# A gated recurrence with ternary weights made beside it: new orders for ScalarE and VectorE, three weight buffers, and a half-width first product

## The chip, the cores and the metric

The kernel runs on one core of a Trainium2 chip. The metric is the device time of one execution in microseconds (us). Five engines work side by side, each through its own instructions in order: TensorE (PE in the profile, PEld for its weight loads), VectorE (DVE), ScalarE (ACT), GpSimd (POOL) and SyncE (SP), which in this kernel issues the DMA transfers. An instruction waits at the head of its engine's queue for what it needs, and all behind it wait too.

## The reference, cut to what matters

`x` is 2 sequences of 1024 tokens with 512 features. Four blocks add to it in turn: a gated recurrence (A), a feed-forward block with ternary weights, a differential attention, and the same feed-forward block again. The change lies in A and in the making of the ternary weights beside it.

```python
def block_a(x, w_in, w_out):                    # x is already layer-normalised
    q, k, v, a, g = split(x @ w_in.T, 5)        # 16 heads of 32
    q = q * rsqrt(mean(q * q, per head) + eps)
    k = tanh(k);  a = clip(sigmoid(a + 2.0), 0.6, 0.9995)
    u = k * v
    # in chunks of 64 tokens, with a state carried from chunk to chunk
    prefix = cumprod(a)
    states = prefix * (state + cumsum(u / max(prefix, 1e-6)))
    gate = sigmoid(g)
    return (gate * (q * states) + (1 - gate) * v) @ w_out.T

def ternary_quant(w):                           # bf16, groups of 64 weights
    scale = clip(mean(abs(w), per group), 1e-8)
    return clip(round(w / scale), -1, 1) * scale

def ffn(x):
    gate, up = split(x @ ternary_quant(w_gate_up).T, 2)
    return rms_norm(silu(gate) * up) @ ternary_quant(w_proj).T

x = x + block_a(layernorm(x));  x = x + ffn(layernorm(x))
x = x + block_b(layernorm(x));  x = x + ffn(layernorm(x))
```

## The kernel before, in words

**Tiles and blocks.** The 2048 tokens lie in the on-chip memory as 16 tiles `x` of 128 tokens by 512 features (`xres[i]` in the code). Stage A (L182 to L430) takes them in four blocks (`NBLK`) of 512 tokens, four tiles each (`TPB`). Per block a tile is normalised (`normal`, giving `xn`), turned by four transposes of TensorE into a bank of PSUM (`transposed`, giving `xnt`), and copied by ScalarE to the block's `a_xt`, features by tokens (`Input.turn`).

**One column group.** Within a block a loop runs over four groups `c` of 128 feature columns. TensorE computes the projections `kv` (with `w_k`, `w_v`) and `ag` (with `w_a`, `w_g`), four matmuls of 128x512 each, into pairs of PSUM banks, two of each kind. ScalarE makes `u`, `v`, `a` and `gate` from them. VectorE and GpSimd then do a chain: clip `a`, the prefix product (a scan), `u` divided by it, the state (a second scan, `mem`), times `qn`, minus `v`, times `gate`, plus `v`, which gives the column `yt`. `qn` is `q` times a factor that TensorE spreads over the heads with one small matmul (`pr`).

**Queries.** `queries` (L273) makes `q` of a block: four products `pq`, each followed by a copy and a square on ScalarE and by a matmul with `headmean` that adds the mean squares up (`pss`); then a root on ScalarE and the reciprocal, split into two parts, on VectorE (`rq_parts`). For the first block this stands ahead of the loop, for the others at the end of the block before. Then 16 matmuls `a_out` with `w_out` give the block's output, four per tile, and VectorE adds each tile's to `x`.

**Ternary weights.** Beside this the feed-forward weights are made ternary in 16 chunks `f` (class `Ternary`, L144): three transfers load a chunk (`w32`), ScalarE takes magnitude and sign (L157, L159), TensorE and ScalarE the mean of each group in three pieces (`mean`, L166 and L167), and VectorE finishes the chunk with six operations of 128x1536 (`finish`, L169 to L179). A transfer then stores it to DRAM (`w_kept`, L319). `quantise(i)` (L310) does piece `i` of the current chunk, 0 to 2 a mean and 3 the finish; the loop calls it at places that a tuple `pieces` lists. After a finish the next chunk is begun: its loads are issued and its magnitude and sign follow. There are two buffers of each kind.

**What follows.** `feed_forward` (L482) reloads all 16 chunks (L569) and takes the first block's normalised and turned tiles as `xs`, in two parts, high and low (class `FeedForwardInput`, L455). Its statistics (`ff_stats`) are taken in the last block of stage A, its tiles turned after it (L570 to L573). The first product is `g` (L524).

**What sets the order.** For TensorE the program's own order holds through stage A (`manual_schedule`, L323); for VectorE only while the first four tiles are normalised (L326). In all other places a scheduler of the framework orders each engine's instructions. SyncE issues transfers in the order it gets, and a transfer that waits holds the queue. Constants are laid by GpSimd in L213 to L240: `headmean`, `headrow`, two `rq_parts` and two `a_start`.

```python
        order = ExitStack()
        order.enter_context(tc.manual_schedule(engines={mybir.EngineType.PE}))
        ...
                if t < NBLK - 1:
                    pieces = ((2,), (), (3,)) if c % 2 else ((0,), (1,), ())
                else:
                    pieces = ((0, 1), (2,), (3,)) if c < NKC - 1 else ((), (), ())
```

Of the kernel before, what the change touches and what calls it, by code (L numbers as in the profile page):

```python
# [10 lines left out]
F32 = mybir.dt.float32  # L11
F32R = mybir.dt.float32r
# [5 lines left out]
P = 128  # L18
D = 512
# [23 lines left out]
def kernel(  # L43
# [37 lines left out]
    def load_x(lo, hi):  # L81
        for i in range(lo, hi):
            nc.sync.dma_start(out=xres[i], in_=x[ts(i, P), :])
# [55 lines left out]


# [3 lines left out]
    class Ternary:  # L144
# [3 lines left out]
        def __init__(self, pool, f, tiles):  # L148
            self.pool, self.f, self.n = pool, f, f"{f}_{tiles[0]}"
            self.shape = [P, len(tiles), D]  # L150
            self.w = pool.tile(self.shape, F32R, tag="w32", name=f"w32_{self.n}")
            w32 = self.w.bitcast(F32)
            for i, e in enumerate(tiles):
                src = w_pt[ts(f, P), :] if e == 2 else w_gu[e * NF + f].rearrange("p c n -> p (c n)")
                nc.sync.dma_start(out=w32[:, i, :], in_=src)
            self.mag = pool.tile(self.shape, BF, tag="mag", name=f"mag{self.n}")
            nc.scalar.activation(self.mag, w32, AF.Abs)  # L157
            self.sign = pool.tile(self.shape, BF, tag="sign", name=f"sign{self.n}")
            nc.scalar.sign(self.sign, w32)  # L159
            self.scale = None  # L160

# [20 lines left out]
    with ExitStack() as s:  # L182
# [15 lines left out]
        w_q, w_k, w_v = (load_w_in(i) for i in range(3))  # L198
# [8 lines left out]
        load_x(TPB, 2 * TPB)  # L207
        w_out = wa.tile([P, NKC, D], F32, name="w_out")
        nc.sync.dma_start(out=w_out, in_=w_out_t.rearrange("(c p) n -> p c n", p=P))

# [20 lines left out]
        for i in range(2):  # L231
            z = wa.tile([P, BLK], F32R, name=f"rq_parts{i}")
            nc.gpsimd.memset(z.bitcast(F32), 0.0)
            rq_parts.append(z)

        a_start = []
        for i in range(2):
            z = wa.tile([P, BLK], F32, name=f"a_start{i}")
            nc.gpsimd.memset(z, 0.0)
            a_start.append(z)  # L240
# [32 lines left out]
        def queries(t, xt):  # L273

            q = ap_.tile([P, NKC, BLK], F32, tag="q", name=f"q{t}")
            pss = bank(f"pss{t}")
            late = []

            def mean_square(c, sq):
                nc.tensor.matmul(  # L280
                    pss, headmean[:, c, :], sq, start=(c == 0), stop=(c == NKC - 1)
                )

            for c in range(NKC):
                pq = bank(f"pq{t}_{c}")
                project(pq, w_q, c, xt)
                nc.scalar.copy(q[:, c, :], pq)
                sq = ap_.tile([P, BLK], F32, tag="sq", name=f"sq{t}_{c}")
                nc.scalar.square(sq, pq)
                if late:  # L290
                    mean_square(*late.pop())
                late.append((c, sq))
                if c < 3 and t:
                    quantise(c)
                elif c and not t:
                    quantise(c - 1)
            mean_square(*late.pop())
            rq = ap_.tile([16, BLK], F32, tag="rq", name=f"rq{t}")
            nc.scalar.activation(rq, pss[:16, :], AF.Sqrt, bias=rms_eps[:16])
            nc.vector.reciprocal(rq, rq)  # L300
            parts = rq_parts[t % 2]
            hi, lo = parts[:16], parts[32:48]
            nc.vector.tensor_copy(hi, rq)
            nc.vector.tensor_sub(lo, rq, hi.bitcast(F32))
            quantise(3)
            return q, parts

        load_x(2 * TPB, NTT)

        def quantise(i):  # L310

            now = chunk[0]
            if now is None:
                return
            if i < 3:
                now.mean(i, bank)
                return
            now.finish(now.w)
            nc.sync.dma_start(out=w_kept[now.f].bitcast(F32), in_=now.w.bitcast(F32))  # L319
            chunk[0] = Ternary(tp, now.f + 1, range(3)) if now.f + 1 < NF else None  # L320

        order = ExitStack()
        order.enter_context(tc.manual_schedule(engines={mybir.EngineType.PE}))  # L323
        before = [None] * NKC
        first = Input(0, at_once=False)
        with tc.manual_schedule(engines={mybir.EngineType.DVE}):  # L326
            for j in range(TPB + 1):
                if j < TPB:
                    first.measure(j)
                if j:  # L330
                    first.normal(j - 1)
                    first.turn(j - 1)
        xt = first.xt
        q, rq = queries(0, xt)
        for t in range(NBLK):
            yt = wa.tile([P, NKC, BLK], F32, tag="yt", name=f"yt{t}")
            following = None
            for c in range(NKC):
                n = f"{t}_{c}"
                kv, ag = big(f"kv{n}"), big(f"ag{n}")  # L340
                project(kv[:, 0, :], w_k, c, xt)
                project(kv[:, 1, :], w_v, c, xt)

                if t < NBLK - 1:
                    pieces = ((2,), (), (3,)) if c % 2 else ((0,), (1,), ())
                else:
                    pieces = ((0, 1), (2,), (3,)) if c < NKC - 1 else ((), (), ())
                for i in pieces[0]:
                    quantise(i)
                project(ag[:, 0, :], w_a, c, xt)  # L350
                project(ag[:, 1, :], w_g, c, xt)
                for i in pieces[1]:
                    quantise(i)
                if following and c > 1:
                    for j in (2 * c - 4, 2 * c - 3):
                        following.turn(j)
# [9 lines left out]
                other = nc.gpsimd if (t, c) < (NBLK - 1, NKC - 1) else nc.vector  # L366
# [12 lines left out]


# [6 lines left out]

                pr = bank(f"pr{n}")
                nc.tensor.matmul(pr, headrow[:, c, :], rq, start=True, stop=True)
                qn = ap_.tile([P, BLK], F32, tag="qn", name=f"qn{n}")  # L390
                nc.vector.tensor_mul(qn, pr, q[:, c, :])
# [4 lines left out]

                if t + 1 == NBLK and c == 0:
                    ff_stats = layernorm_stats(range(TPB), "f0_0")
                if t + 1 < NBLK and c < 2:
                    if c == 0:  # L400
                        following = Input(t + 1)
                    following.normal(0 if c == 0 else 1)
                for i in pieces[2]:
                    quantise(i)
                if following and c == 2:
                    following.normal(2)
                    following.normal(3)

            if following:
                xt = following.xt  # L410
                q_next, rq_next = queries(t + 1, xt)
            products = [(j, k) for j in range(TPB) for k in range(NKC)]
            if not following:

                order.close()
                products.sort(key=lambda jk: jk[1] == NKC - 1)
            po = {}
            for j, k in products:
                if k == 0:
                    po[j] = bank(f"a_out{t}_{j}")  # L420
                nc.tensor.matmul(
                    po[j], yt[:, k, ts(j, P)], w_out[:, k, :], start=(k == 0), stop=(k == NKC - 1)
                )
                if k == NKC - 1:
                    xi = xres[t * TPB + j]
                    nc.vector.tensor_add(xi, xi, po[j])
                    if following:
                        quantise(j)
            if following:
                q, rq = q_next, rq_next  # L430

    edge_sb = ctx.enter_context(tc.tile_pool(name="edge", bufs=1, reuse_waits="tile"))
# [20 lines left out]
    class FeedForwardInput:  # L455


        def __init__(self, which, t, pool, tag, stats=None):
            self.n = f"{which}_{t}"
            self.which, self.tiles = which, range(t * TPB, (t + 1) * TPB)  # L460
            self.stats = stats or layernorm_stats(self.tiles, f"f{self.n}")
            self.xs = pool.tile([P, 2, NKC, BLK], F32R, tag=tag, name=f"xs{self.n}", bufs=1)
            self.xn = {}

        def normal(self, j):
            i = self.tiles[j]
            self.xn[j] = normal(i, j, self.stats, f"f{self.which}_{i}")

        def tile(self, j, psum):
            if j not in self.xn:  # L470
                self.normal(j)
            pt = transposed(self.xn.pop(j), f"f{self.which}_{self.tiles[j]}", psum)
            hi, lo = (self.xs[:, e, :, ts(j, P)] for e in range(2))
            nc.scalar.copy(hi, pt)  # L474
            nc.vector.tensor_sub(lo, pt, hi.bitcast(F32))

# [5 lines left out]
    def feed_forward(which, store, first=None, beside=None):  # L482


        with ExitStack() as s:
# [84 lines left out]
            if not first:  # L570
                first = FeedForwardInput(which, 0, edge_sb, "xt", ff_stats)
                for j in range(TPB):
                    first.tile(j, ring)  # L573
# [44 lines left out]
        0, False, None,  # L618
# [533 lines left out]
```

## Time and profile before

| | us |
|---|---|
| time, median of 3 runs | 2147.88 (2146.33 to 2148.32) |
| time of the profiled execution | 2146.65 |
| its span | 2144.9 |
| mean granted clock of TensorE in it | 0.996 of full speed |

By stretches the trace has, in microseconds busy:

| stretch | TensorE | VectorE | ScalarE | GpSimd |
|---|---|---|---|---|
| 0 to 20, first tiles | 11.79 | 6.88 | 6.29 | 5.76 |
| 20 to 90, queries and block 0 | 67.58 | 48.39 | 36.05 | 17.38 |
| 90 to 165, block 1 begins | 74.00 | 52.12 | 30.46 | 13.93 |
| 165 to 240 | 71.85 | 48.31 | 34.97 | 14.32 |
| 240 to 316 | 74.27 | 56.69 | 29.95 | 22.35 |
| 316 to 400, last block | 77.04 | 62.41 | 25.49 | 17.87 |
| 400 to 2144, all the rest | 1732.23 | 794.25 | 672.00 | 358.19 |

The span runs from the first instruction of the profiled execution to its last; the execution's own time has some two microseconds around it. A stretch is read by holding an engine's busy time against its length: TensorE lacks 8.2 us in the first, 2.4 in the second, 7.0 in the last of stage A. What ended such a gap is in the view of waits, which names the instruction that waited and the one that released it. An engine's busy time says nothing of whether anyone waits for it.

### The profile page before, as it was taken

What the parts mean: (1) busy time and instruction counts of PE and PEld (TensorE: products, weight loads), DVE (VectorE), ACT (ScalarE), POOL (GpSimd) and SP (SyncE); (2) the same over time, 40 slices, a digit from 0 to 9 for tenths busy, and PEclk for the clock granted to TensorE, in tenths of its full rate; (3) what the DMA queues carried; (4) which work ended last, traced back from release to release, by engine and by line L of the source; (5) the groups of instructions that cost most, each with busy time, mean ns of one, the idle gap of its engine ahead of it and who ended that gap; (6) DMA issues with size and microseconds to landing.
All of it is one profiled execution on the core that took longest, in us unless ns stands there. A gap on an engine that the chain in (4) does not pass through costs nothing.

```text
span 2144.9 us, 28054 instructions
## 1 busy us (share of the span) xinstructions
PE 2108.8 (98%) x10615; PEld 1242.2 (58%) x10624; DVE 1069.1 (50%) x2272; ACT 835.2 (39%) x1590; POOL 449.8 (21%) x812
## 2 busy tenths in 40 slices
PE   8999999999999999999999999999999999999998
PEld 3444444688888854444444444444545447888887
DVE  5766686533343234555555465464546662433322
ACT  4444333234344322444444422243434523333333
POOL 1312212122122221111111113021212221121212
PEclk9999999999999999999999999999999999999999
DMA  6111211600000111111110101201110033000000
GB/s 255 59 59 62 86 59 74 250 1 1 1 1 1 35 46 37 41 26 41 23 44 21 46 8 37 57 20 42 24 32 15 14 111 132 20 1 20 1 20 20
DMA packets 50999, 98.71 MB, mean 46 GB/s; under 512 B 10800, under 2 KB 19120, under 8 KB 50864
## 3 DMA queue, kind: packets, MB, share of 16 engines
q1 hardware_dynamic: 50864, 96.93, 13.8%
q8 instruction: 83, 1.36, 0.3%
q14 instruction: 52, 0.43, 0.1%
HBM read 58.75 MB, written 16.78 MB: 35 GB/s over the span
## 4 chain that ended last, share of the span: by engine, by line
PE 83%; DVE 8%; DMA 4%; ACT 2%; issue 1%; POOL 1%; SPq 1%; DVEq 0%; ACTq 0%; POOLq 0%
PE y L904 12%; PE g L524 11%; PE u L524 11%; PE f_out L545 11%; PE s L805 10%; PE pq L737 8%; PE t L866 8%; PE pv L702 3%; PE b_out L965 2%; DMA w<-in_w_pt_dram 1%; DMA w_kept<-w 1%; DVE one L174 1%; PE kv L269 1%; DVE w L179 1%; PE ag L269 1%
## 5 line engine op out<-in xcount | busy, mean ns | idle before, releaser
L882 ACT ACTIVATE pr<-t 128x512 f32<-128x512 f32 (+3 forms) x768 | 314.8, 497 | 380.6 <-PE t L874 380.4
L815 DVE CUSTOM_DVE_ANT_0 s<-s,causal 128x128 f32<-128x128 f32 (+3 forms) x512 | 245.3, 510 | 126.1 <-PE s L805 117.4
L904 PE MATMUL y<-pr,val 128*64 128x512 f32 (+3 forms) x1536 | 291.6, 501 | 0.2 <-POOL pr L885 0.2
L539 POOL TENSOR_TENSOR ssq<-ssq,sq 128x512 f32<-128x512 f32 x120 | 155.9, 1299 | 603.6 <-ACT sq L538 603.6
L530 DVE TENSOR_TENSOR h<-h,u 128x512 f32<-128x512 f32 x128 | 88.0, 688 | 362.0 <-PE u L524 355.9
L524 PE MATMUL g<-xs,w 128*128 128x512 f32 x1024 | 262.4, 398 | 0.9 <-ACT xs L474 0.7
L545 PE MATMUL f_out<-w,hs 128*128 128x512 f32 x1024 | 257.7, 394 | 0.3 <-DVE hs L533 0.3
L820 DVE TENSOR_REDUCE nmax<-s 128x1 f32<-128x512 f32 x256 | 165.0, 686 | 184.4 <-PE s L805 184.3
L524 PE MATMUL u<-xs,w 128*128 128x512 f32 x1024 | 256.4, 392 | 0.0
L805 PE MATMUL s<-gr,gr 32*128 32x512 f32 (+3 forms) x1536 | 248.8, 492 | 2.6 <-DVE nmax L815 2.6
L524 PEld LDWEIGHTS u<-xs,w 128*128 128x128 f32 x1024 | 192.4, 188 | 43.5
L545 PEld LDWEIGHTS f_out<-w,hs 128*128 128x128 f32 x1024 | 191.6, 188 | 43.9 <-DVE hs L533 1.1
L524 PEld LDWEIGHTS g<-xs,w 128*128 128x128 f32 x1024 | 190.9, 189 | 44.0 <-ACT xs L474 0.9
L866 PE MATMUL t<-gr,gr 32*128 32x512 f32 (+3 forms) x1536 | 198.8, 533 | 0.0
L904 PEld LDWEIGHTS y<-pr,val 128*64 128x64 f32 x1536 | 93.5, 136 | 179.9 <-issue 105.7
L737 PE MATMUL pq<-b_xt,w_qk 128*128 128x512 f32 x384 | 176.0, 603 | 0.0
L805 PEld LDWEIGHTS s<-gr,gr 32*128 32x128 f32 x1536 | 147.6, 185 | 46.8 <-issue 14.0
L532 ACT CAST hs<-h 128x512 fp32r<-128x512 f32 x128 | 79.4, 621 | 236.6 <-DVE h L530 236.6
L885 POOL TENSOR_SCALAR_AFFINE_SELECT pr<-pr 128x256 f32<-128x256 f32 x256 | 101.3, 408 | 332.2 <-ACT pr L882 332.2
L529 ACT ACTIVATE h<-g 128x512 f32<-128x512 f32 x128 | 76.5, 598 | 224.3 <-PE g L524 224.1
L533 DVE TENSOR_TENSOR hs<-h,hs 128x512 fp32r<-128x512 f32 x128 | 88.6, 692 | 83.1 <-ACT hs L532 83.1
L737 PEld LDWEIGHTS pq<-b_xt,w_qk 128*128 128x128 f32 x384 | 69.6, 189 | 88.0 <-issue 74.0
(155 smaller groups left out, 2211.0 us busy)
## 6 DMA issues: line engine op xcount, KB each, us to landing
w<-w_kept SPq DMA_DIRECT2D x32, 768.0 KB, 8.7
w_kept<-w SPq DMA_DIRECT2D x16, 768.0 KB, 3.2
gr<-gr SPq DMA_DIRECT2D x96, 128.0 KB, 2.3
w<-in_w_gu_dram SPq DMA_DIRECT2D x32, 256.0 KB, 2.8
share<-ys SPq DMA_DIRECT2D x128, 64.0 KB, 2.0
w_in<-in_w_in_t_dram SPq DMA_DIRECT2D x5, 1024.0 KB, 11.2
x<-in_x_dram SPq DMA_DIRECT2D x16, 256.0 KB, 7.1
w<-in_w_pt_dram SPq DMA_DIRECT2D x16, 256.0 KB, 3.5
```

The source lines that it names most:

```text
L524: nc.tensor.matmul(po, ws[f][:, part, ts(k, P)], xs[:, e, k, :], start=(k == 0 and e == 0), stop=(k == NKC - 1 and e == 1),)
L533: nc.vector.tensor_sub(hp[:, 1, :], h, hp[:, 0, :].bitcast(F32))
L539: nc.gpsimd.tensor_add(ssq, ssq, sq)
L545: nc.tensor.matmul(po[j], hp[:, e, ts(j, P)], ws[f][:, 2, :], start=(f == 0 and e == 0), stop=(f == NF - 1 and e == 1),)
L737: nc.tensor.matmul(po, w[:, k, ts(kind, P)], xts[b][:, k, ts(e, BLK)], start=(k == 0), stop=(k == NKC - 1),)
L805: nc.tensor.matmul(part, queries[:, ts(j, P)], keys[:, first : first + nk], start=True, stop=True,)
L815: nc.vector.tensor_tensor_reduce(part, part, causal[:, BLK - part.shape[-1] :], -1.0, 3.0e38, ALU.add, ALU.min, top,)
L820: nc.vector.tensor_reduce(top, part, AX.X, ALU.max, negate=True)
L866: nc.tensor.matmul(banks[u, e][:, :nq], keys[:, ts(kb, P)], queries[:, (qb + 1) * BLK - nq : (qb + 1) * BLK], start=True, stop=False,)
L882: nc.scalar.activation(pr[:, e, :nq], banks[u, e][:, :nq], AF.Exp)
L885: nc.gpsimd.affine_select(out=pr[:, :, :P], in_=pr[:, :, :P], compare_op=ALU.is_ge, fill=0.0, base=0, pattern=[[0, 2], [1, P]], channel_mu ...
L904: nc.tensor.matmul(y[64 * e : 64 * e + 64, lo:], all_values[:, HV * (NH * kb + h) : HV * (NH * kb + h) + 64], pr[:, e, : BLK - lo], start= ...
```

## The change

1. **VectorE's order.** Through all of stage A the program's order now holds for VectorE as well as for TensorE, until the stage's end. To suit it, the text is rearranged: the tiles of the next block are turned before `w_a`, not after `w_g`; `pr` and `qn` stand before the second scan; `qn` is written over `q`; the normals of the next block stand in the chain.
2. **The first four tiles.** ScalarE's order is given there instead of VectorE's own block. The first product of queries is made in two halves of 256 tokens; the first matmul of it stands before the fourth tile is turned.
3. **Constants.** `rq_parts` and `a_start` are set by VectorE instead of GpSimd.
4. **Three buffers of ternary weights.** `Ternary` is split: the loads come with the object, magnitude and sign with `begin`. Chunks 0, 1 and 2 are loaded at the start, chunk 1 ahead of `w_out`, chunk 2 behind it; chunk `f + 3` is loaded when `f` is finished. The loads of tiles 8 to 15 of `x` come after the first queries.
5. **Queries in parts.** The last mean square and the root (`roots`) and the reciprocal (`factors`) are called later, behind other products.
6. **The end of the stage.** The first feed-forward block's input is made inside the last block: nine statistics and two normals after column 1 (`c == 1`), the turns around `w_a` of column 3. Chunk 15's finish, and so its store, comes after all products. `w_q` and `w_k` share the memory that `xs` takes later. The 16 products of the last block are sorted by `max(k, 1)`.

```diff
+            self.w = pool.tile(self.shape, F32R, tag="w32", name=f"w32_{self.n}", bufs=3)
...
+        def begin(self):
+            pool, w32 = self.pool, self.w.bitcast(F32)
...
+        w_qk = edge_sb.tile([P, 2, NKC, D], F32, tag="xt", name="w_in_qk")
+        w_q, w_k = w_qk[:, 0], w_qk[:, 1]
...
+        chunk.append(Ternary(tp, 1, range(3)))
         w_out = wa.tile([P, NKC, D], F32, name="w_out")
         nc.sync.dma_start(out=w_out, in_=w_out_t.rearrange("(c p) n -> p c n", p=P))
+        chunk.append(Ternary(tp, 2, range(3)))
...
-            nc.gpsimd.memset(z.bitcast(F32), 0.0)
+            nc.vector.memset(z.bitcast(F32), 0.0)
...
-            nc.gpsimd.memset(z, 0.0)
+            nc.vector.memset(z, 0.0)
...
-            chunk[0] = Ternary(tp, now.f + 1, range(3)) if now.f + 1 < NF else None
+            chunk.pop(0)
+            if chunk:
+                chunk[0].begin()
+            if now.f + 3 < NF:
+                chunk.append(Ternary(tp, now.f + 3, range(3)))
...
-        order.enter_context(tc.manual_schedule(engines={mybir.EngineType.PE}))
+        fixed = {mybir.EngineType.PE, mybir.EngineType.DVE}
+        order.enter_context(tc.manual_schedule(engines=fixed))
...
+        def begin(half, k):
+            cols = ts(half, BLK // 2)
+            nc.tensor.matmul(
+                begun[:, cols], w_q[:, k, :P], first.xt[:, k, cols],
+                start=(k == 0), stop=(k == NKC - 1),
+            )
+
+        with tc.manual_schedule(engines={mybir.EngineType.Activation}):
             for j in range(TPB + 1):
                 if j < TPB:
                     first.measure(j)
                 if j:
                     first.normal(j - 1)
                     first.turn(j - 1)
+                if j == 3:
+                    begin(0, 0)
+        for k in range(1, NKC):
+            begin(0, k)
+        for k in range(NKC):
+            begin(1, k)
+        chunk[0].begin()
...
+                if not last:
                     pieces = ((2,), (), (3,)) if c % 2 else ((0,), (1,), ())
                 else:
-                    pieces = ((0, 1), (2,), (3,)) if c < NKC - 1 else ((), (), ())
+                    pieces = (((0, 1), (2,), (3,)), ((0, 1), (2,), ()), ((), (), ()))[max(c - 1, 0)]
+                project(kv[:, 0, :], w_k, c, xt)
+                if t + c == 0:
+                    roots()
+                    factors()
+                project(kv[:, 1, :], w_v, c, xt)
+                if t + c == 0:
+                    quantise(3)
+                if not last and c > 1:
+                    for j in (2 * c - 4, 2 * c - 3):
+                        following.turn(j)
+                        if c == 2:
+                            following.normal(j + 2)
                 for i in pieces[0]:
                     quantise(i)
+                ff_tiles = range(TPB) if last and c == NKC - 1 else ()
+                turn = lambda name: bank(name)
+                for j in ff_tiles[:2]:
+                    ff_first.tile(j, turn, j + 2)
                 project(ag[:, 0, :], w_a, c, xt)
+                for j in ff_tiles[2:]:
+                    ff_first.tile(j, turn)
                 project(ag[:, 1, :], w_g, c, xt)
...
                 other.tensor_add(yt[:, c, :], mem, v)
...
                 for i in pieces[2]:
                     quantise(i)
...
+                if last and c == NKC - 3:
+                    ff_first = FeedForwardInput(0, 0, edge_sb, "xt")
+                    ff_first.normal(0)
+                    ff_first.normal(1)
...
-                products.sort(key=lambda jk: jk[1] == NKC - 1)
+                products.sort(key=lambda jk: max(jk[1], 1))
...
                     nc.vector.tensor_add(xi, xi, po[j])
-                    if following:
+                    if not last:
+                        if j == 0:
+                            roots()
+                        elif j == 1:
+                            factors()
                         quantise(j)
-            if following:
+            if last:
+                quantise(3)
+            if not last:
                 q, rq = q_next, rq_next
+                following = Input(t + 2) if t + 2 < NBLK else None
+        order.close()
```

## The prediction

> **What bounds the kernel now.** The page comes first. TensorE is busy for nearly the whole span, so only what changes its work, its waits or its clock can move the time.
>
> ```profile
> PE 2108.8 (98%) x10615; PEld 1242.2 (58%) x10624; DVE 1069.1 (50%) x2272; ACT 835.2 (39%) x1590; POOL 449.8 (21%) x812
> ```
>
> The changed program's instruction order after the first `g` product equals the old one but for a few semaphore waits, so only the first 400 us matter. The view of waits for TensorE over 0 to 420 us lists what can be won there (total, times, longest):
>
> ```profile
> PE xnt_a L136 <- DVE xn_a L127: 7.5, 3, 6.8
> PE pm L166 <- ACT mag L157: 4.7, 2, 2.7
> PE pss L280 <- ACT sq L289: 3.4, 5, 2.1
> PE pq L269 <- ACT a_xt L265: 2.6, 4, 0.7
> PE xnt_f L136 <- DVE xn_f L127: 2.3, 2, 1.9
> PE a_out L421 <- POOL yt L395: 1.0, 1, 1.0
> ```
>
> About 23 us in all, 6.8 of them the unavoidable first load. VectorE's 50% is a mean: the view by stretches has it at 32.8 of 40 us in 360 to 400. The third resource is SyncE's queue, which issues in order. Its timeline around the stage's end, and TensorE's:
>
> ```profile
> 361.89 15.17 SPq L319 DMA_DIRECT2D w_kept<-w  x2
> 377.17 19.11 SPq L569 DMA_DIRECT2D w<-w_kept  x16
> ```
>
> ```profile
> 392.43 1.02 PE L421 MATMUL a_out<-w_out,yt 128*128 128x512 f32 x2
> ...
> 398.59 0.50 PE L524 MATMUL g<-xs,w 128*128 128x512 f32 x1 [0.68 <-ACT xs L474]
> ```
>
> The reader should see that the first ternary weights are asked for at 377.2, right behind the last store (376.7), and so are there long before `g` needs them at 398.6. The DMA view of that stretch gives 5.6 us from issue to landing for the first load.
>
> **Start.** VectorE takes over four memsets of 128x512. None is in the trace there: from its 128x1 (0.06 us) and 128x64 (0.11) each is about 0.49, an estimate; POOL's same memset took 0.52. Four end near 3.5 us, as the first `x` lands (3.56), and cost nothing; were they twice as long, the start would slip by 2 us. Off POOL they stop disturbing the first `xn_a`:
>
> ```profile
> 5.35 1.32 DVE L127 TENSOR_SCALAR xn_a<-x,mv_a,rstd_a 128x512 f32<-128x512 f32 x1
> 5.41 0.98 POOL L239 MEMSET a_start<- 128x512 f32 x2
> ```
>
> The median of these is 0.55, so the transposes begin 0.77 earlier. ScalarE's order lets copies 0 and 1 pass `rstd` 2 and 3, but the half product then meets its weights: `w_in0`, issued at 2.67, landed 7.6 later, at 10.3. So: first half matmuls 10.3 to 11.15, the fourth tile's transposes to 12.15, then 14 half matmuls. Before, `pq` began at 12.38; five matmuls took 0.855 and the rest 0.43, so its first column ended near 17.95. The slow rate lasted 4.4 us. If it lasts 4.4 from 10.3, six halves at 0.43 and eight at 0.215 end at 16.4: **1.6 us won**. The Trainium skill, "TensorE: Matmul & The Clock Gate" (Part 1), says that the window of 3.4 us is free-running; then the slow rate ends 3.4 to 6.8 us after the start, and the gain is 2.0 to 0.4. I take the row, and the rule for the range.
>
> **Middle.** Turning tiles before `w_a` removes the wait for `a_xt` at three block ends (0.63, 0.64, 0.63 in TensorE's timeline). The last mean square now stands behind a product: 4 waits of 0.32. With three buffers and chunks 1 and 2 loaded ahead of `w_out`, chunk 1's `mag` is no longer late (2.06 at 39.9); the 16 later transfers of `x` give way, and nobody needs them for 60 us. The waits of 2.07 (203.7) and 0.68 (295.2) also come from ScalarE's queue holding a `mag` whose load was late. Together 8.0 us.
>
> Against it stands VectorE's written order. One chunk's finish, from its timeline:
>
> ```profile
> 110.76 0.56 DVE L171 TENSOR_SCALAR scale<-scale 128x1536 bf16<-128x1536 bf16 x1 [4.44 <-ACT scale L167]
> 111.36 1.76 DVE L174 SCALAR_TENSOR_TENSOR one<-scale,mag 128x1536 bf16<-128x1536 bf16 x1
> 113.15 0.96 DVE L176 TENSOR_TENSOR scale<-scale,mag 128x1536 bf16<-128x1536 bf16 x1
> 114.14 0.96 DVE L177 TENSOR_TENSOR scale<-scale,mag 128x1536 bf16<-128x1536 bf16 x1
> 115.14 0.96 DVE L178 TENSOR_TENSOR scale<-scale,one 128x1536 bf16<-128x1536 bf16 x1
> 116.13 1.76 DVE L179 TENSOR_TENSOR w<-scale,sign 128x1536 fp32r<-128x1536 bf16 x1
> ```
>
> That is 7.1 us undisturbed, 7.9 at the stage's means. A column's chain (clip, scan, factors, scan, two products) is 7.9 from the busy times of its rows and its two waits for POOL (0.75 and 1.4), which the scheduler used to fill with pieces of the other and which now stand idle. At each of the first three block ends VectorE does: last chain, ended 8.7 after `ag`; a finish, 7.9; a wait of 2.1 for ScalarE (which holds `mag` until that finish lets its buffer go); a second finish, 7.1; only then the first `x` addition, 0.7. Sum 26.5. TensorE reaches the matmul that needs the bank this addition frees after 0.43 + 4x3.43 + 3x(0.86+0.21) + 2x3.43 + 1.07 = 25.3. So it waits about 1.2, 3.7 for three ends. **Middle: 4.3 won**, between 8.0 (VectorE quicker by 1.3) and about nothing.
>
> **Last block, the centre of the sum.** TensorE's work from its first `kv` to the last `a_out`, transposes included, is 8x6.87 + 9x0.21 + 4x0.43 + 4x0.52 + 32x0.43 = 74.4. In the trace this stretch plus waits runs from 316.13 to 398.59: 82.5. New, counted from its start:
> - VectorE gets `a` of column 0 at 15.1. Then in fixed order: chain 7.9, chunk 13's finish 7.9, chain 7.9, chunk 14's finish 7.9, nine statistics 7.0 (0.8 a pair at 23 us), reciprocal and two normals 1.3. The second normal is ready at 55.0; TensorE wants the first at 51.3.
> - Column 2's chain with one statistic, 9.1, then normal 0.55, `xs` 0.69, normal 0.55: 65.9. TensorE needs these for tiles 2 and 3, between `w_a` and `w_g`; `w_g` starts at 66.5 instead of 56.8: **9.7 lost**. ScalarE, POOL and `yt` queue behind the same chain but are not later than TensorE.
> - `w_g`, `pr` and 32 products: 17.6, to 84.1. `yt` of the last column comes at 78.9, in time for the four products that now stand last; the old wait of 1.0 is gone.
> - Chunk 15's finish now stands behind the last `x` addition: 0.1 + 0.69 + 7.1 + a statistic 0.66 = 8.6, to 92.7. SyncE's queue has that chunk's store ahead of all 16 weight loads, and the store waits. Store and issue 0.6, landing 5.6: `g` starts at 98.9. **14.8 of waiting**, covered before by the store having gone out 17 us earlier.
>
> 98.9 against 82.5 is 16.4 lost. The earlier `xnt_f` and `xs` waits are in the 82.5.
>
> **Clock.** The granted clock by stretches, around a wait of 2.7 us (352.4 to 355.1) and one of 1.95 (to 397.3); it is the third number from the end, before the DMA share and GB/s:
>
> ```profile
> 354.00:356.00 2.00, 0.94 (x3) 0.57 (x3) 1.82 (x3) 2.00 (x2) 0.90 (x1) 0.68 0.00 0
> 356.00:358.00 2.00, 2.00 (x4) 0.88 (x3) 1.01 (x1) 2.00 (x5) 0.95 (x1) 0.50 0.04 8
> ```
>
> The reader should see 0.68 and 0.50: half speed for some 3 us. It cost 1.1 us in `ag` (8.17 for 7.03) and 2.2 at `g` (eight matmuls in 4.07 for 1.87). The same page of the skill (the table "Why this matters") warns only of gaps above about 3 us; here gaps of 2 to 2.7 did it, so the trace decides. By the rule the new waits (3.2, 5.5) give one slow window, 1.7; by the row 2.2. I take **2.0**. The 14.8 gives another at `g`, where one was already.
>
> Sum: -1.6 - 4.3 + 16.4 + 2.0 = **+12.5**. On the profiled execution's 2146.65 (span 2144.9 and 1.75 around it) that is 2159; the median shown is 1.2 higher, 2160.4. I say 2160.
>
> **Rivals.** A measurement here tells some 0.2% (4.3 us) from no change.
> - *VectorE is not late at the end.* Speaks for it: it idled a third of most stretches. Against: before, chain plus finish took 15.2 to 15.9 us per column there (ends at 348.7, 364.5, 379.8), already interleaved. Without the 9.7 and the 2.0: +0.8, about 2148. Chance 0.11.
> - *The weight loads don't stand behind the store.* Place: SyncE's queue after chunk 14; it decides as soon as one load is issued before the last `x` addition. Price: 14.8 and the slow `g` (2.2) gone: -4.5, 2143, faster. Against: the order is fixed in the program, and 361.9 to 376.7 shows this queue waiting 14.4 us for VectorE. Chance 0.07.
> - *VectorE is also late in blocks 1 and 2*, so that finishes contend with POOL (one 2.70 and scale 1.49 where POOL ran, 88 to 93): 8.9 per finish instead of 7.9 adds about 2 per block end and 2 at the end: +20, 2168. Chance 0.14.
> - *The half product does nothing*, for its weights land late: +14, inside the forecast's range.
>
> Forecast 0.68. Its own range, with the last block's VectorE 10% quicker to 8% slower, and the bounds above, is 2152 to 2167; 2150 to 2168 holds 8 in 10. Slower 0.82, same 0.11, faster 0.07.
>
> **What would show it.** Right: `pq` with 256 columns from about 10.3; no wait of `pm` for `mag` near 40; `w_kept` and the 16 loads issued only after the last `a_out`, a gap of 13 to 16 us before `g`, and waits of `xnt_f` on `xn_f` of some 8 to 10 in all. Wrong: loads issued before the last addition, or `xnt_f` without waits.

## The result, and the profile after

The changed kernel takes 2163.68 us (median of 4 runs, 2161.07 to 2166.22), the kernel before 2147.57 beside it. The ratio is 1.0076, with a 95% interval of 1.0058 to 1.0093: slower by 16 us. The profiled execution took 2163.43, its span 2161.7, at a mean granted clock of 0.992 (0.996 before).

Four stretches make up the span, cut at places that both programs pass, each read from TensorE's timeline (the second query product ends where the first `pss` starts):

| stretch | before | after | difference | predicted |
|---|---|---|---|---|
| start to the end of the second query product | 21.53 | 19.25 | -2.28 | -1.6 |
| from there to the last block's first `kv` | 294.60 | 294.99 | +0.39 | -4.3 |
| from there to the first `g` | 82.46 | 101.38 | +18.92 | +18.4 (16.4 and clock 2.0) |
| from there to the end of the span | 1746.31 | 1746.08 | -0.23 | 0 |

The view of TensorE's waits over 0 to 420 us (total, times, longest), after the change:

```profile
PE g L583 <- DMA w<-w_kept: 14.4, 1, 14.4
PE xnt_f L136 <- DVE xn_f L127: 10.0, 3, 7.3
PE xnt_a L136 <- DVE xn_a L127: 7.5, 3, 6.0
PE a_out L496 <- ACT rq L344: 3.6, 3, 1.3
PE pm L196 <- DVE x L501: 2.9, 3, 1.0
PE pss L320 <- ACT sq L330: 0.6, 3, 0.2
```

The waits for `mag`, for `a_xt` and for `yt` are gone, as intended. Four others have come or grown, and 24.4 us of them lie in the last block. There VectorE's timeline (start, duration) reads:

```profile
357.05 2.71 DVE L204 SCALAR_TENSOR_TENSOR one<-scale,mag 128x1536 bf16<-128x1536 bf16 x1
359.79 1.91 DVE L206 TENSOR_TENSOR scale<-scale,mag 128x1536 bf16<-128x1536 bf16 x1
...
371.26 0.67 DVE L109 BATCH_NORM_STATS2 st_f<-x 128x6 f32<-128x512 f32 x1
371.84 0.99 DVE L127 TENSOR_SCALAR xn_f<-x,mv_f,rstd_f 128x512 f32<-128x512 f32 x2
```

and TensorE's and SyncE's:

```profile
372.43 1.97 PE L136 MATMUL xnt_f<-ident,xn_f 128*128 128x128 f32 x8 [7.32 <-DVE xn_f L127]
374.19 5.63 PE L308 MATMUL ag<-a_xt,w_in 128*128 128x512 f32 x8
381.79 0.66 PE L136 MATMUL xnt_f<-ident,xn_f 128*128 128x128 f32 x4 [1.97 <-DVE xn_f L127]
...
415.62 3.75 PE L583 MATMUL g<-xs,w 128*128 128x512 f32 x8 [14.37 <-DMA w<-w_kept]
```

```profile
346.37 63.45 SPq L361 DMA_DIRECT2D w_kept<-w  x3
409.93 13.41 SPq L628 DMA_DIRECT2D w<-w_kept  x13
```

VectorE is busy without a break from chunk 14's finish through all the statistics, and only then makes the normals that TensorE has been waiting for since 365. Of the nine statistics there the program's text asks for four at this place; ScalarE's root of these four is ready at 369.47, and its reciprocal comes on VectorE only at 371.18, behind statistics of later blocks. So some 1.7 of the 7.3 is not chunk 14's finish. The eight products after that wait run slow (5.63 for 3.60). SyncE's three stores, the last waiting for chunk 15's finish, hold its queue from 346 to 410; the first reload goes out at 409.93 and `g` starts 5.7 later.

### The profile page after: what moved, and what is told of

It is laid out like the page before. It is cut to its first block, busy times and chain, and to the rows that moved or that the text cites. A ratio compares the mean times of both kernels' runs of the same rounds, so it can differ in the third digit from the quotient of the medians.

```text
span 2161.7 us, 28045 instructions
## 1 busy us (share of the span) xinstructions
PE 2109.4 (98%) x10623; PEld 1245.4 (58%) x10632; DVE 1079.1 (50%) x2276; ACT 833.4 (39%) x1588; POOL 448.7 (21%) x808
## 4 chain that ended last, share of the span: by engine, by line
PE 90%; DVE 5%; DMA 2%; ACT 1%; POOL 1%; issue 1%; SPq 1%; DVEq 0%; ACTq 0%; POOLq 0%
PE y L959 12%; PE g L583 11%; PE u L583 11%; PE f_out L604 11%; PE s L860 10%; PE pq L792 8%; PE t L921 8%; PE ag L308 4%; PE kv L308 4%; PE pv L757 3%; PE b_out L1020 2%; PE a_out L496 2%; PE mt L900 1%; PE t L929 1%; DVE one L204 1%; DMA w<-w_kept 1%
## 5 line engine op out<-in xcount | busy, mean ns | idle before, releaser
L583 PE MATMUL g<-xs,w 128*128 128x512 f32 x1024 | 262.3, 398 | 14.4 <-DMA w<-w_kept 14.4
```

Source lines behind the costliest of these rows:

```text
L583: nc.tensor.matmul(po, ws[f][:, part, ts(k, P)], xs[:, e, k, :], start=(k == 0 and e == 0), stop=(k == NKC - 1 and e == 1),)
```

## The experiments

The times are medians; the kernel before, run beside them, took 2147.7 to 2148.1.

**e1, the last store on another queue.** Edit, in `quantise`:

```diff
+            queue = nc.gpsimd if now.f == NF - 1 else nc.sync
-            nc.sync.dma_start(out=w_kept[now.f].bitcast(F32), in_=now.w.bitcast(F32))
+            queue.dma_start(out=w_kept[now.f].bitcast(F32), in_=now.w.bitcast(F32))
```

> The changed kernel, but chunk 15's store is issued from GpSimd's queue, so that SyncE's queue goes straight from chunk 14's store to the weight loads. My theory: the 14.4 us that `g` waits in the changed kernel is SyncE's queue standing at that store, for the first load itself needs only memory that is free some 100 us earlier. Then the wait of `g` for `w<-w_kept` falls to under 1 us, its slow first product (3.75 for 2.06) becomes fast, and the waits of `xnt_f` stay at 10.0: 2163.7 - 14.4 - 1.7 = about 2147.5. Rival: the load waits for memory that stage A still holds, or for the channel; then the wait of `g` stays over 10 us and the time over 2159.

Measured: 2152.83 (ratio 1.0023, 1.0013 to 1.0034), 10.9 below the changed kernel. Its view of waits:

```profile
PE xnt_f L136 <- DVE xn_f L127: 10.8, 3, 7.3
...
PE f_out L605 <- ACT hs L592: 2.1, 1, 2.1
```

No wait of `g` is left, and `g` takes 2.42 instead of 3.75. So the store in SyncE's queue was the cause, and the loads needed no memory that was late. The expected 2147.5 was not reached: chunk 15's finish still stands on VectorE ahead of the first `h`, so the first `f_out` waits 2.1 and the `g` after it runs slow (3.02 for 2.03).

**e2, chunk 15's finish after column 2, VectorE's order kept.**

```diff
-                    pieces = (((0, 1), (2,), (3,)), ((0, 1), (2,), ()), ((), (), ()))[max(c - 1, 0)]
+                    pieces = (((0, 1), (2,), (3,)), ((0, 1), (2,), (3,)), ((), (), ()))[max(c - 1, 0)]
...
-            if last:
-                quantise(3)
```

> The changed kernel, but chunk 15's finish stands after column 2 of the last block instead of after the last product; VectorE's order stays given. My theory: VectorE has no spare time there, so the end is paid elsewhere: the wait of `g` (14.4) goes, but the normals of tiles 2 and 3 and the last column's chain come later by the finish, 7.1 to 9, and TensorE waits for `xnt_f` 17 to 19 us instead of 10.0. Time 2163.7 - 14.4 + 8 = about 2157. Rival, that the finish fits into idle stretches of VectorE: the waits of `xnt_f` stay within 2 us of 10 and the time is about 2149.

Measured: 2159.56 (ratio 1.0053, 1.0034 to 1.0072; its profiled execution, 2153.58, was its fastest). The wait of `g` is gone, and this stands in its place:

```profile
PE xnt_f L136 <- DVE xn_f L127: 17.3, 2, 10.0
```

So the theory held: the waits of `xnt_f` grew by 7.3, and half of the 14.4 came back. VectorE has no room there. The other three executions took 2159.4 to 2160.5, and why they are 6 slower than the traced one is open.

**e3, VectorE's order free; e6, free but for the first four tiles.**

```diff
-        fixed = {mybir.EngineType.PE, mybir.EngineType.DVE}
+        fixed = {mybir.EngineType.PE}
...
-        with tc.manual_schedule(engines={mybir.EngineType.Activation}):
+        with tc.manual_schedule(engines={mybir.EngineType.Activation, mybir.EngineType.DVE}):
```

The second pair of lines is e6's alone.

> The changed kernel, with VectorE's order left to the scheduler (one word taken out of the set of fixed engines); TensorE's order, the buffers and the rearranged text stay. The scheduler then puts chunk 15's finish ahead of the last column's last products. My theory: the given order of VectorE is what costs at the end and at the block ends; waits of `xnt_f` fall from 10.0 to under 4, the wait of `g` from 14.4 to under 3, the waits of `pm` for the addition to `x` (2.9) go in the main: 2138 to 2145, faster than before. Rival: VectorE's total work in the last block is what is late, in whatever order; then the waits of `xnt_f` or of `a_out` stay at 8 or more in all and the time is 2147 or more.

> As e3 (VectorE's order free), but for the first four tiles VectorE's order is given besides ScalarE's. In e3 the first transposes began at 7.76 instead of 5.95, since the scheduler put all four statistics ahead of the first normal, and the second query product ended 1.3 later. Theory: these 1.3 come back: 2143.2 - 1.3 = about 2142. Rival: the load of the first weights, which lands near 10.3, sets the start, and nothing is gained: 2143.2.

Measured: e3 2143.23 (ratio 0.9979, 0.9972 to 0.9986), e6 2140.62 (0.9964, 0.9951 to 0.9978). Both beat both kernels. The view of waits of e3:

```profile
PE xnt_a L136 <- DVE rstd_a L116: 7.8, 1, 7.8
PE pss L320 <- ACT sq L330: 5.8, 2, 4.8
PE xnt_f L136 <- DVE xn_f L127: 4.3, 2, 2.5
PE xnt_a L136 <- DVE xn_a L127: 0.9, 1, 0.9
```

`g`, `pm` and `a_out` wait no more. The instructions of TensorE are the changed kernel's, one for one; only VectorE's order, with what the scheduler makes of it on ScalarE and GpSimd, differs. So the lateness in the last block was the order, not the amount of work: from its first `kv` to the first `g` e3 takes 79.18, the changed kernel 101.38. In e6 the second query product ends at 19.12, in e3 at 20.51: the order of the first tiles is worth the 1.4 of the 2.6 between the medians; where the rest lies was not found.

**e11, VectorE's order given in the kernel before**, and nothing else changed.

> The kernel before, with VectorE's order given through stage A and nothing else changed. Theory: a given order of VectorE costs by itself, since a finish of 7 us then stands ahead of each column's next chain or addition to `x`, and chains and finishes no longer fill each other's waits for GpSimd (2.1 us a column); the last column's `yt` comes late: 2147.9 + 6 to 14, 2154 to 2162, with waits of `a_out` for `yt` or of `pm` and `kv` for banks of 5 us or more. Rival: the order alone is harmless, and only what was moved in the last block (chunk 15's finish, the turned tiles) costs: 2144 to 2152.

Measured: 2171.17 (ratio 1.0107, 1.0093 to 1.012), 23 us slower and more than I expected; and through another wait than the ones I named. Its view of waits, and ScalarE's timeline at the longest:

```profile
PE pm L166 <- ACT mag L157: 22.9, 5, 11.3
```

```profile
377.26 1.48 ACT L157 ACTIVATE mag<-w 128x1536 bf16<-128x1536 f32 x1 [8.58 <-DMA w<-in_w_pt_dram]
```

Of 22.9, 4.7 was there before: 2.06 near 40, and 2.68 where it is now 11.3. With two buffers a late finish makes a late load, and that a late magnitude. From the changed kernel to e6 it is 23.1 us as well, but by other waits: there 22.2 lie in the last block (101.38 against 79.18), here 9.5 (91.93 against 82.46) and the rest at the block ends. That the sums are equal is chance; that a given order of VectorE costs holds in both arrangements of the text.

**e4 and e12, the root at the block ends.** The third `a_out` of each end waits for a bank that the root `rq` reads. ScalarE's timeline of the changed kernel shows why the root is late:

```profile
113.58 1.48 ACT L186 ACTIVATE mag<-w 128x1536 bf16<-128x1536 f32 x1 [4.83 <-DMA w<-in_w_pt_dram]
115.08 1.28 ACT L344 ACT_TABLE_LOAD   x1
116.38 0.68 ACT L344 ACTIVATE rq<-pss,rms_eps 16x512 f32<-16x512 f32 x1
```

The scheduler had put a magnitude, whose load was still under way, ahead of it. e4 called `roots()` right after the queries; e12 gave ScalarE's order while the three ends' `a_out` are made:

```diff
             po = {}
+            with ExitStack() as given:
+                if not last:
+                    given.enter_context(tc.manual_schedule(engines={mybir.EngineType.Activation}))
```

> The changed kernel, but at the block ends the last mean square and the root come right after the queries, not after the first `a_out`. In the changed kernel ScalarE's root stands behind a magnitude whose load is not there (it waits 4.8 us), and the third `a_out` needs the bank that this root reads: 1.2 us at each of three ends. Theory: these three waits (3.65) go, three waits of about 0.3 for the square come back, and the slow clock at one end (about 1.6) goes: 2163.7 - 4.3 = about 2159.5. Rival: the next wait (for the first addition to `x` behind two finishes) takes their place, since VectorE is late there anyway: the waits of `pm` for `x` grow from 2.9 to about 6 and the time stays within 1.5 of 2163.7.

> The changed kernel, VectorE's order still given, with ScalarE's order given too while the three block ends' `a_out` are made, so that the root comes ahead of the magnitude that the scheduler had put before it; e4 tried to take this wait away and made another. Theory: the three waits of `a_out` for `rq` (3.65) go, the waits of `pm` for the addition to `x` (2.9) stay, and the slow clock at a block end (about 1.6) goes where it was: 2163.7 - 3.6 to 5.2 = 2158.5 to 2160. Rival: the root was only last in a chain that VectorE's two finishes hold up, and the third `a_out` then waits for a bank that the addition to `x` frees: the waits of TensorE at the three ends stay at 6 or more in all and the time at 2162 or more.

e4: 2167.83 (ratio 1.0097, 1.0082 to 1.0112), 4 slower. Both its theory and its rival missed: the last mean square, now without a product ahead of it, waits 2.14 three times for a square, and runs slow after it. The change had hidden that wait, for which I had counted 0.32. e12: 2157.67 (ratio 1.0046, 1.0029 to 1.0063), 6.0 better than the changed kernel. Its waits for `rq` are gone, those of `pm` are the same 2.9, and the last block's first `kv` comes 6.1 sooner (e12, then the changed kernel):

```profile
308.18 3.60 PE L308 MATMUL kv<-a_xt,w_in_qk 128*128 128x512 f32 x8
```

```profile
314.24 3.60 PE L308 MATMUL kv<-a_xt,w_in_qk 128*128 128x512 f32 x8
```

**e5, the first product whole.**

```diff
-                if j == 3:
-                    begin(0, 0)
-        for k in range(1, NKC):
-            begin(0, k)
-        for k in range(NKC):
-            begin(1, k)
+        project(begun, w_q, 0, first.xt)
```

> The changed kernel, but the first product of queries is made whole, after the fourth tile is turned. Theory: of the 2.3 us by which the changed kernel has its second query product earlier (19.25 against 21.53), 0.9 comes from the earlier transposes (5.95 against 6.82) and the rest from the half product, which starts the slow rate of TensorE's clock sooner; so here that point comes at about 20.6, with the first matmul of `pq` near 11.5 to 12, and the time is 2163.7 + 1.4 = about 2165. Rival: the half product does nothing, since its weights land at 10.3 and the clock needs its time anyway; then the point stays within 0.4 of 19.25 and the time at 2163.7.

Measured: 2168.27 (ratio 1.0092, 1.0078 to 1.0105). TensorE's timeline of e5, then of the changed kernel:

```profile
12.20 9.58 PE L308 MATMUL pq<-a_xt,w_in_qk 128*128 128x512 f32 x16 [0.68 <-ACT a_xt L304]
21.62 1.02 PE L320 MATMUL pss<-sq,headmean 128*128 128x512 f32 x2
```

```profile
10.70 1.19 PE L378 MATMUL pq<-a_xt,w_in_qk 128*128 128x256 f32 x2
...
19.25 1.02 PE L320 MATMUL pss<-sq,headmean 128*128 128x512 f32 x2
```

The point comes at 21.62, where the kernel before has it (21.53). So all of the start's gain, 2.4, is the half product, and the earlier first transposes bring nothing by themselves: both theory and rival missed. Other traces agree: with the half product and the first tiles in order the point lies at 17.8 to 19.3 in nine traces (e7 is left out, where this matmul waits 1.48), with the whole product at 21.5 to 21.9 in three. The span of e5 is 4.2 longer than the changed kernel's, and the other 1.8 lie at the block ends: this execution's third wait for `rq` was 2.27, with `a_out` slow after it (6.52 for 3.60).

**e8, two buffers on e6.** Loads and magnitude of a chunk are issued when the one before is finished, as before the change.

> As e6, but with two buffers of ternary weights, each chunk's load issued and its magnitude begun when the chunk before is finished, as before the change. Theory: the three buffers are worth the waits that the kernel before has for late magnitudes (2.06 near 40, 2.07 near 204, 0.68 near 295): waits of `pm` for `mag` or of `pss`, `pq` behind a late `mag` add 3 to 5 us, 2145 to 2147. Rival: with the other edits the loads are no longer what holds ScalarE up, and it makes under 1 us: 2142 to 2143.

Measured: 2149.83 (ratio 1.0008, 1.0000 to 1.0016), 9.2 slower than e6, twice what I expected. The wait of 2.06 near 40 is back; `pss` and `ag` wait 9.3 at five places (5.4 at two in e6), and `xnt_f` waits 6.8 instead of 4.4. The third buffer is worth more here than the waits for `mag` that the kernel before shows; how much of it comes through ScalarE's queue and how much through VectorE's later finishes was not taken apart.

**e7, e9, e10, towards a better version.** All start from e6. e7 gives ScalarE's order through stage A; e9 only around `queries` and the finish after it at a block end; e10 adds to e9 that tiles 2 and 3 of the feed-forward input are turned after `w_g`.

```diff
+                with tc.manual_schedule(engines={mybir.EngineType.Activation}):
                     q_next, rq_next, roots, factors = queries(t + 1, xt)
                     quantise(3)
```

> As e6, but ScalarE's order is given through stage A instead of VectorE's. In e3 TensorE waited 4.8 and 1.1 us at two block ends for a square of the queries (`sq`), which stood on ScalarE behind a magnitude that the scheduler had put ahead and that waited 11.9 us for a finish of VectorE. Theory: with the program's order that magnitude stands behind the queries, both waits go and with them the slow clock behind the first (1.5): 2142 - 7 = about 2135. Rival: a given order brings new waits, as VectorE's did (magnitudes and roots at the head of ScalarE's queue): waits of TensorE for ScalarE of 5 us or more in all, and 2142 or more.

> As e6, but ScalarE's order is given only within the next block's queries at a block end (copies, squares, means and the magnitude that follows them), not through the stage as in e7. In e6 a square of the queries stood behind a magnitude that waited 11 us for a finish: TensorE waited 4.4 and 1.1 us at two block ends and ran slow after the first (two `pss` in 2.07 for 1.02, a `pq` of 8 in 4.73 for 3.60). Theory: with the magnitude kept behind the squares these go: 2140.6 - 5.4 - 2.2 = about 2133. Rival: the magnitude then comes too late for its means, and `pm` waits for `mag` as long, or slots of the kind seen in e7 open elsewhere: 2139 or more.

> As e9, and the third and fourth tile of the feed-forward input are turned after `w_g` instead of between `w_a` and `w_g`. In e6 TensorE waits 1.9 and 2.5 us there for the normals, and its next product runs slow. Theory: 3.4 us of products come first, so both waits go in the main, and 3 to 5 us are won: about 2129. Rival: VectorE is the bound there, since the last column's chain starts no sooner; the wait then moves to `a_out` for the last `yt`, and under 1.5 us are won.

e7: 2157.32 (ratio 1.0041, 1.0029 to 1.0054). The rival held, and by a wait that was not there before:

```profile
PE kv L308 <- ACT v L439: 19.8, 9, 2.8
```

At the first of these, ScalarE's `u` and `v` (48.21, 48.70), which free the banks of `kv`, stand behind the copy of a mean that TensorE makes only after `w_g` (at 45.91), and the next `kv` waits for them. e9: 2136.09 (ratio 0.9946, 0.9934 to 0.9959), 4.5 won of the 7.6 expected. With the square on time, the same `pss` still waits, now for VectorE, and the products after it are slow (5.45 for 3.60):

```profile
98.38 2.05 PE L320 MATMUL pss<-sq,headmean 128*128 128x512 f32 x2 [2.95 <-DVE a_start L450]
```

```profile
97.55 0.68 DVE L462 TENSOR_TENSOR q<-pr,q 128x512 f32<-128x512 f32 x1
98.15 0.17 DVE L450 COPY a_start<-a 128x8 f32<-128x8 f32 x1
```

The view names the copy `a_start`, which reads nothing from PSUM. I take it that the bank was freed by the product `q` just ahead of it, done at 98.2 behind a finish (89.1 to 97.3). In the traces `g` starts at 390.73 in e6 and 389.29 in e9; the other 3.2 by which e9's span is shorter lie after `g`, in work that e9 leaves alone. That last stretch takes 1744.7 to 1747.9 in all traces but e1's, so of the 4.5 only 1.4 is shown to come from the edit. e10: 2135.85 (0.9942, 0.9929 to 0.9956), the same as e9. Its rival held (under 1.5 won), though the wait that came is another one than named:

```profile
PE a_out L497 <- DVE xs L164: 3.4, 1, 3.4
```

By their medians e9 and e10 are 12 us faster than the kernel before and 28 faster than the changed one.

## Why the prediction held, point by point

- **The weight loads behind the last store** (14.8 predicted): 14.4, and e1 shows that the place in SyncE's queue made it. Right.
- **VectorE late in its given order** (9.7): 10.0, and e3 shows that it is the order. The sum was right and its split was not, so part of this agreement is luck. I had the first normal 3.7 late and the third some 6; it was 7.3 and 2.7. Two finishes took 9.0 each and not 7.9 (`one` 2.70, a `scale` 1.91, while GpSimd worked). That is the 8.9 that I gave to a rival for blocks 1 and 2, and it happened here. TensorE, held longer ahead of `w_a`, then waited less ahead of `w_g`.
- **Clock** (2.0): in the last block 2.0 in `ag` and 0.9 in the transposes, 2.9. The row of the trace (2.2), not the page's rule of some 3 us (1.7), gave the nearer number, though the longest wait here is above both. The 2.2 was itself read too high: 4.07 runs to the end of the eighth matmul and holds a wait of 0.24, 1.87 runs from start to start. Read alike, the eight took 3.65, 1.8 too long.
- **Start** (-1.6): -2.28, just beyond the range's 2.0. The mechanism was right, and e5 shows that the half product makes all of it. But the slow rate ended sooner than my row had it. The 14 half matmuls took 3.28 from start to start, where 14 at 0.215 make 3.0, so it was over near 13.1, some 2.4 after the first half matmul (10.70); in e5 it lasted some 5.1. These are estimates from the durations: the granted clock reads 1.00 there in both programs. My estimate of 3.4 to 6.8 from the page's window doesn't hold 2.4, and why it was short is open.
- **Middle** (-4.3): +0.39, and this is the step that failed. The 8.0 of waits did go. I sized the new wait of `pm` at 3.7 and it is 2.9. But I took "the last mean square now stands behind a product" as gain alone and left out the root that comes after it: its place on ScalarE behind a hoisted magnitude, whose chunk's load follows a late store, costs 3.65 in the view of waits, and one of these waits was followed by half clock, which cost 1.6. e12 shows the whole price: with the root ahead of the magnitude this stretch takes 289.00, 6.0 less than in the changed kernel and 5.6 less than in the kernel before. Squares still wait 0.6. In waits that is 8.8 against 8.0, or +0.8, where the trace has +0.39. Most of the difference is in how a wait is counted: from start to start of the matmuls around it, a wait costs 0.15 to 0.27 more than its idle time, and there were ten before and nine after. Counted so, it is 10.8 against 10.5.
- **The size**: 16.8 measured on the spans against 12.5; the missing 4.3 is nearly all the middle's 4.7. The time, 2163.7, lies in the forecast's own range. With the root put right (e12) the span is 11.0 above the kernel before.
- **The rivals**: "VectorE is not late" and "the loads don't stand behind the store" fell with the first two points. "The half product does nothing" fell with e5. "Also late in blocks 1 and 2" did not come at the block ends: the waits of `pm` for the addition are 2.9, below the 3.7 that I had without it.

## What to carry to other kernels

A given order on an engine with 7 us pieces and 0.7 us pieces makes the short ones wait for the long one ahead of them, and cost 23 us in both arrangements here; fix the order where a few instructions must come first (the first tiles here, the queries in e9), and leave the rest free. Before the end of a stage, ask which store is the last in the queue that the next stage loads through. A buffer that lets loads run ahead can be worth more than the waits it is seen to remove (9.2 against 4.8 here). And before a gain is credited to an edit, see in which stretch it lies (e9).

## What the runs showed of the hardware that was not expected

TensorE's clock fell after shorter waits than the prediction's rows had, and not each time. At the three block ends of the changed kernel the waits of `a_out` are 1.16, 1.23 and 1.26; only the second was followed by half clock. The view by stretches (the granted clock is the third number from the end), after the second and after the third:

```profile
212.00:214.00 2.00, 2.00 (x3) 0.67 (x2) 2.00 (x1) 1.60 (x2) 0.00 (x0) 0.50 0.15 46
```

```profile
307.00:309.00 2.00, 1.94 (x5) 0.99 (x6) 1.96 (x1) 2.00 (x4) 0.00 (x0) 1.00 0.24 98
```

Each stands behind a wait of 0.97 (0.98 at the second) with only one `pm` between, so the idle time adds up to 2.1 to 2.2 us. In the kernel before, the prediction's 1.95 was likewise the longest of four waits within 5 us (0.36, 1.95, 0.68, 0.24), while a wait of 2.07 near 205 left the granted clock at 1.00. So neither the length of the wait nor the sum decides. The rule of the Trainium skill's page "TensorE: Matmul & The Clock Gate" that the prediction used, gaps above about 3 us, does not cover these. The free-running window of that page (Part 1) could make it a matter of where in a window the idle time falls; that is not shown, and no run was made for it.

VectorE and GpSimd hold each other up. `one` took 2.70 instead of 1.76, and GpSimd's product of `u` and `v` 2.78 instead of 1.27. In order of time, GpSimd and VectorE:

```profile
337.55 1.45 POOL L476 TENSOR_TENSOR yt<-mem,v 128x512 f32<-128x512 f32 x1 [0.87 <-DVE mem L475]
338.96 2.78 POOL L446 TENSOR_TENSOR u<-u,v 128x512 f32<-128x512 f32 x1
```

```profile
337.92 2.70 DVE L204 SCALAR_TENSOR_TENSOR one<-scale,mag 128x1536 bf16<-128x1536 bf16 x1
340.65 1.91 DVE L206 TENSOR_TENSOR scale<-scale,mag 128x1536 bf16<-128x1536 bf16 x1
```

`one` ends 1.62 after `yt` ended (339.00), the product 1.12 after `one` ended (340.62), `scale` 0.82 after the product ended (341.74). Near 357 the same four stand in the same row, with the same three distances. That looks like taking turns, each held until the other's instruction is done, and not like both running slower side by side; no run was made to separate the two.
